# A four-layer graph network on one core: layer 0 issued in single tiles over six block periods, and layers 1 and 3 without split products

## The chip, the cores and the metric

The kernel runs on one core of a Trainium2 chip. The metric is the device time of one execution in microseconds (us), as the median of several runs. The core has five engines that run side by side, each with a queue of its own that it works through in order: TensorE (PE in the profile; its weight loads are PEld), VectorE (DVE), ScalarE (ACT), GpSimd (POOL) and SyncE (SP). DMA transfers are issued from a queue (SP's, or GpSimd's for gathers) and run on 16 DMA engines.

## What is computed

The input is `x`, 2708 nodes of 512 features, and `adj`, a 2708 x 2708 matrix that is nearly empty: a diagonal, and some four other positive entries in a row. Four layers follow one another, each with a residual and a layer normalisation over the 512 features:

```python
x = layernorm(x + (x - (adj @ x) * (diag + 1)) @ W0 + b0)                        # layer 0
x = layernorm(x + sigmoid(gate_a * ((attn @ x) @ W_sa) + gate_b * ((adj @ x) @ W_gc + b)))  # layer 1
x = layernorm(x + ((adj + head) @ x) / rowsum(adj + head))                       # layer 2
x = layernorm(x + tanh((d * (adj + I) * d) @ x @ W3.T + b3))                     # layer 3
```

`attn` is a softmax-like weighting of the same edges (an exponential of leaky scores, divided by its row sum), the gates are sigmoids of sums over the same edges, `head` is a row-normalised mask of them, and `d` is the inverse square root of the column sums. All four layers thus sum neighbours' rows with weights on the same edges. The gates' sums and the scores are linear in `x`, so six extra columns beside each row carry what they need.

## The kernel before

The nodes are cut into 22 blocks of 128 rows (the last has 20). A block of the matrix is loaded transposed, so that a column is a row of `adj`. Layer 0 finds the edges, keeps them for the later layers as a list, and uses them; each block has up to 5 tiles of 128 edges (the last block 1).

**Layer 0**, for a block, in steps (lines 828 to 1052): `load_adj` brings the block's 2708 x 128 matrix into one of two buffers (SP, line 767); `mask` clears the diagonal (GpSimd, 838); `negatives` sums negative entries (ScalarE, 843, two halves); `find` takes the 8 largest values and their places in each of five segments (VectorE, 858 and 859); `number`, `offsets`, `spans`, `places` number the edges; `select` makes a 0/1 matrix on GpSimd (893); `spread_rows` multiplies it on TensorE so that each edge gets its row of candidates (`got`, 904); `keep_rows` copies it out (ScalarE, 917); `pick_edges` picks the edge's value and its neighbour's index (VectorE, 925 to 962); `pick_rows` makes `pick`, a 0/1 matrix in bf16 that says which edge belongs to which row (GpSimd, 971 and 973); `gather_x` fetches the neighbours' rows of `x` by five indirect DMAs (GpSimd, 598) into one of two buffers `xg`; `weigh` multiplies `pick` by the edge values (VectorE 620, its diagonal tile ScalarE 626); `l0_aggregate` sums the rows with these weights on TensorE (995); `add_bias` (GpSimd, 983), `l0_residual` (1002), `l0_u` (VectorE, 1007), a transpose, its copy (680) and `l0_project` (688) give the layer's output; `l0_stats`, `l0_std`, `l0_rstd` and `l0_norm` normalise it (ScalarE's Sqrt at 1026); `x1_transpose`, `x1_copy` and `x1_columns` make the extra columns and store block and columns (SP, 740).

The order is written out by hand. `steps` (1059) gives each step a time within a block, block i is shifted by i times `STEP` = 15, and all steps of all blocks are issued in the order of the sums. These numbers are no waits: they only order each engine's queue, and a semaphore holds an instruction until its data and its buffer are there. A block's steps span 73 units, from the matrix load at -15.5 to the columns at 57.7, all five gathers stand together (26.1), and so do four of the five tile products (35.1).

**Layers 1 to 3** have a common loop (`layer`, 1214): gather the next block, prepare its weights, compute the present block, finish the one before. There a scheduler orders the queues. Layer 1 also gathers one score for each edge (`sl`, line 1121), exponentiates (1142) and makes two weightings of the same rows: `l1a` with the edge values and `l1e` with the attention. Both are transposed and projected with `w_gc` and `w_sa` into one accumulator `l1o` (1199 to 1201).

In layers 1 and 3 most tiles are not multiplied as float32. `split_rows` (634) scales a gathered tile by its edge values into `hi`, rounded to fp32r (ScalarE, 637), and puts the rest into `lo` (VectorE, 639); `picked` (644) makes an fp32r copy of `pick`; `aggregate` (652) then multiplies `pick` by `hi` and by `lo`, two products for a tile:

```python
products = [(s[:, nt, :r], xs[:, i, :D])]
products += [(s[:, t, :r], tiles[:, t, :D]) for t in range(len(parts), nt)]
products += [(pick_s[:, t, :r], x_) for t, pair in enumerate(parts) for x_ in pair]
```

`SPLIT_A, SPLIT_E, SPLIT_3 = 5, 3, 4` are the tiles that are split in `l1a`, `l1e` and `l3a`. The other tiles and the diagonal's are float32 products, as are all of layer 2's. The norms of layers 1 to 3 (`layernorm`, 728) take the inverse root on VectorE by an estimate and two refining steps (`rsqrt`, 710), and layer 1's sigmoids are written with Tanh (1179 and 1207).

## Time and profile before

| What | Value |
|---|---|
| Runs shown | 1240.12, 1244.64, 1236.41 us; median 1240.12 |
| The profiled execution's own time | 1240.12 us |
| Its span, first to last instruction | 1238.4 us, clock 0.918 |
| Busy: TensorE, VectorE, ScalarE, GpSimd | 986.6, 834.2, 524.4, 744.5 us |
| Layer 0's last product (line 1098) starts | 481.4 us |
| Layer 1's projections (`l1o`) | 541.2 to 871.9 us |
| Layer 2's first gathered product, last block's residual (line 1305) | 884.4, 1030.6 us |
| Layer 3's last norm input (line 1346) | 1227 us |

The page lists busy times by engine, then the span in 40 slices, then the chain of work that ended last, then groups of instructions by line. A group gives its count, its busy time, the mean of one, and the idle time of the engine just before it with what ended that. In the order of time of one engine, the bracket behind an instruction is the wait before it and what released it. A float32 matmul stands in the records as two instructions.

### The profile page before, as it was taken

How to read it: one execution, taken by the hardware profiler on the slowest of the kernel's cores; microseconds unless marked ns; L12 is line 12 of the kernel's file. 1: busy time of each engine (PE TensorE's matmuls, PEld its weight loads, DVE VectorE, ACT ScalarE, POOL GpSimd, SP SyncE). 2: the span in 40 equal slices, each digit the busy share in tenths (PEclk: the TensorE clock that was granted, in tenths of full speed). 3: DMA queues.
4: the chain of work that ended last, by engine and by line, in shares of the span. 5: the costliest groups of instructions: out<-in, count | busy, mean ns of one | idle time of the engine just before them, and what ended most of it. 6: DMA issues, size and time to landing. Idle time of an engine off the chain costs nothing.

```text
span 1238.4 us, 12921 instructions
## 1 busy us (share of the span) xinstructions
PE 986.6 (80%) x3074; PEld 502.7 (41%) x3074; DVE 834.2 (67%) x2661; ACT 524.4 (42%) x1033; POOL 744.5 (60%) x787
## 2 busy tenths in 40 slices
PE   0478787777787785379999999999788885799996
PEld 0244344344444442145545555554223332355552
DVE  3677567678566653647767777774487785688885
ACT  1234243343333321446666666664111212666652
POOL 5565565666465642777777777720477775777730
PEclk9989788989788887589999999999899997999998
DMA  8467887787778524222323322310466664566521
GB/s 221 128 119 167 130 168 148 160 138 147 157 146 143 98 51 81 56 78 86 88 80 87 85 83 86 86 54 18 122 185 189 196 197 133 160 198 181 174 90 38
DMA packets 119692, 153.24 MB, mean 124 GB/s; under 512 B 25996, under 2 KB 82864, under 8 KB 119608
## 3 DMA queue, kind: packets, MB, share of 16 engines
q0 software_dynamic: 39024, 95.21, 31.2%
q1 hardware_dynamic: 78472, 57.12, 19.6%
q8 instruction: 26, 0.43, 0.2%
q14 instruction: 58, 0.48, 0.1%
q10 hardware_dynamic: 2112, 0.01, 0.1%
HBM read 152.03 MB, written 22.23 MB: 141 GB/s over the span
## 4 chain that ended last, share of the span: by engine, by line
PE 34%; DMA 15%; issue 7%; DVE 5%; ACT 4%; POOL 3%; POOLq 0%; ACTq 0%; DVEq 0%
PE l1o L688 12%; DMA xg<-x2d,ej 5%; PE l2a L661 5%; PE l1e L661 5%; PE l3o L688 4%; DMA xg<-in_x_dram,ej 3%; DMA xg<-x1d,ej 3%; DMA xg<-x3d,ej 3%; PE l1a L661 2%; POOL xg L598 2%; PE l0a L995 2%; PE l3a L661 2%; ACT hi_s L637 1%; POOL sl L598 1%; DMA x1d<-xs 1%
## 5 line engine op out<-in xcount | busy, mean ns | idle before, releaser
L995 PE MATMUL l0a<-xg,s 128*128 128x512 f32 x212 | 132.4, 749 | 59.8 <-DMA xg<-in_x_dram,ej 59.8
L598 POOL DMA_INDIRECT sl<-sld,er x106 | 127.0, 1199 | 54.0 <-issue 25.6
L598 POOL DMA_INDIRECT xg<-x2d,ej x106 | 114.6, 1081 | 42.5 <-issue 18.0
L598 POOL DMA_INDIRECT xg<-x3d,ej x106 | 114.8, 1083 | 41.5 <-issue 15.8
L598 POOL DMA_INDIRECT xg<-x1d,ej x106 | 110.7, 1044 | 47.2 <-issue 18.9
L598 POOL DMA_INDIRECT xg<-in_x_dram,ej x106 | 111.2, 1049 | 29.1 <-issue 20.8
L661 PE MATMUL l2a<-xg,s2i 128*128 128x512 f32 x212 | 110.3, 638 | 19.2 <-DMA xg<-x2d,ej 18.5
L688 PE MATMUL l1o<-w_gc_sb,uT_l1a 128*128 128x512 f32 (+1 forms) x176 | 88.0, 629 | 15.3 <-ACT uT_l1a L680 15.0
L688 PE MATMUL l3o<-w_sb,uT_l 128*128 128x512 f32 (+1 forms) x176 | 82.6, 613 | 9.4 <-ACT uT_l L680 8.6
L858 DVE MAX8 found<-adj 128x8 f32<-128x512 f32 (+1 forms) x110 | 80.4, 731 | 13.0 <-POOL adj L838 13.0
L995 PEld LDWEIGHTS l0a<-xg,s 128*128 128x128 f32 x212 | 43.8, 234 | 110.1 <-issue 55.5
L639 DVE SCALAR_TENSOR_TENSOR lo_s<-xg,ev,hi_s 128x512 fp32r<-128x512 f32 x85 | 62.9, 743 | 32.6 <-ACT hi_s L637 32.5
L639 DVE SCALAR_TENSOR_TENSOR lo_a<-xg,ev,hi_a 128x512 fp32r<-128x512 f32 x106 | 77.8, 739 | 7.6 <-ACT hi_a L637 5.8
L688 PE MATMUL l0o<-w_sb,uT_l 128*128 128x512 f32 (+1 forms) x176 | 81.3, 604 | 0.7 <-ACT uT_l L680 0.7
L637 ACT ACTIVATE hi_a<-xg,ev 128x512 fp32r<-128x512 f32 x106 | 71.6, 712 | 23.9 <-DMA xg<-x1d,ej 20.8
L859 DVE FIND_INDEX8 index<-found,adj 128x8 uint32<-128x512 f32 (+1 forms) x110 | 81.3, 739 | 0.0
L688 PE MATMUL l1o<-w_sa_sb,uT_l1e 128*128 128x512 f32 (+1 forms) x176 | 79.1, 592 | 0.0
L661 PEld LDWEIGHTS l2a<-xg,s2i 128*128 128x128 f32 x212 | 37.6, 194 | 88.1 <-DMA xg<-x2d,ej 63.7
L904 PE MATMUL got<-found,sel 128*128 128x120 f32 x212 | 41.5, 365 | 36.7 <-POOL sel L893 30.7
L637 ACT ACTIVATE hi_s<-xg,ev 128x512 fp32r<-128x512 f32 x85 | 59.2, 715 | 21.9 <-DMA xg<-x3d,ej 20.4
L893 POOL TENSOR_SCALAR sel<-sel,count 128x640 f32<-128x640 f32 (+1 forms) x22 | 40.8, 1855 | 45.5 <-DVE st_l L698 31.8
L971 POOL CAST ec<-row 128x5 f32<-128x5 uint32 (+1 forms) x22 | 4.1, 189 | 103.2 <-DVE row L954 103.2
(235 smaller groups left out, 2210.9 us busy)
## 6 DMA issues: line engine op xcount, KB each, us to landing
adj<-in_adj_dram SPq DMA_DIRECT2D x21, 1344.0 KB
x1d<-xs SPq DMA_DIRECT2D x21, 257.5 KB
xs<-in_x_dram SPq DMA_DIRECT2D x21, 256.0 KB
x2d<-xs SPq DMA_DIRECT2D x21, 256.0 KB
x3d<-l2y SPq DMA_DIRECT2D x21, 256.0 KB
out_dram<-y SPq DMA_DIRECT2D x21, 256.0 KB
xg<-in_x_dram,ej POOLq DMA_INDIRECT x106, 8.6
xg<-x1d,ej POOLq DMA_INDIRECT x106, 3.6
```

The source lines that it names most:

```text
L598: nc.gpsimd.indirect_dma_start(out=dst, out_offset=None, in_=src[:, :], in_offset=bass.IndirectOffsetOnAxis(ap=index, axis=0), bounds_chec ...
L637: nc.scalar.activation(hi, tiles[:, t, :D], AF.Copy, scale=v)
L639: nc.vector.scalar_tensor_tensor(lo, tiles[:, t, :D], v, hi, op0=ALU.mult, op1=ALU.subtract)
L661: nc.tensor.matmul(agg[:r, :], lhsT=w, rhs=x_, start=k == 0, stop=k == len(products) - 1)
L688: nc.tensor.matmul(o[:r, :], lhsT=uT[:, f, :r], rhs=w[:, f, :], start=start and f == 0, stop=stop and f == DB - 1,)
L858: nc.vector.max(out=best, in_=part)
L859: nc.vector.max_index(index[:, i, 8 * s : 8 * s + 8], best, part)
L893: nc.gpsimd.tensor_scalar(sel[i][:, :m], sel[i][:, :m], count[i][:, SLOTS - 1 : SLOTS], None, op0=ALU.is_lt)
L904: nc.tensor.matmul(got[i][:, t // per_bank, k : k + 3 * SLOTS], lhsT=sel[i][:, t * P : (t + 1) * P], rhs=found[i].rearrange("p a s -> p (a ...
L971: nc.gpsimd.tensor_copy(ec[:, :nt], row[i][:, :nt])
L995: nc.tensor.matmul(agg[i][:r, :], lhsT=weights[i][:, t, :r], rhs=rhs, start=t == 0, stop=t == nt)
```

## The change

Layer 0's table of steps is written anew. `STEP` becomes 15.81 and a block's steps span 105.5 units. Steps are taken apart so that each queue can order them by itself: `gather_x` and `l0_aggregate` are called for one tile at a time, the ScalarE copies of `offsets`, `spans` and `x1_columns` become `keep_offsets`, `keep_values` and `keep_columns`, and the diagonal tile of `weigh` becomes `weigh_diagonal`. Each still does the same. `load_adj` stands at 0 and `mask` directly behind it at 0.1. `select` is issued on VectorE instead of GpSimd. No buffer count of layer 0 changes.

In layers 1 and 3 `split_rows` and `picked` go: every tile is a float32 product with weights from `weighted`. `layernorm` takes ScalarE's Sqrt and VectorE's reciprocal in place of `rsqrt`, and layer 1's two sigmoids are ScalarE's Sigmoid. Left out of the diff below are constants, the names of dictionaries, and the call sites of `l1_compute` and `l3_compute`, which no longer pass the split parts.

```diff
@@ -611,56 +604,40 @@
...
-    def weighted(i, vals, pool, name, diag=None, first=0):
+    def weighted_edges(s, i, vals):
+        r = rows(i)
+        nt = n_tiles(i)
+        nc.vector.tensor_tensor(
+            s[:, :nt, :r],
+            pick[:, i, :nt, :r],
+            vals[:, :nt, None].to_broadcast([P, nt, r]),
+            ALU.mult,
+        )
+    def weighted_diagonal(s, i, vals):
+        r = rows(i)
+        nt = n_tiles(i)
+        nc.scalar.activation(s[:, nt, :r], ident[:, :r], AF.Copy, scale=vals[:, nt : nt + 1])
+    def weighted(i, vals, pool, name, diag=None):
         r = rows(i)
...
         s = pool.tile([P, TILES + 1, P], FP, tag="s", name=name)
-        if first < nt:
-            nc.vector.tensor_tensor(
-                s[:, first:nt, :r],
-                pick[:, i, first:nt, :r],
-                vals[:, first:nt, None].to_broadcast([P, nt - first, r]),
-                ALU.mult,
-            )
-        nc.scalar.activation(
-            s[:, nt, :r],
-            ident[:, :r],
-            AF.Copy,
-            scale=vals[:, nt : nt + 1] if diag is None else diag,
-        )
+        weighted_edges(s, i, vals)
+        if diag is None:
+            weighted_diagonal(s, i, vals)
+        else:
+            nc.scalar.activation(s[:, nt, :r], ident[:, :r], AF.Copy, scale=diag)
         return s
-    def split_rows(pool, tiles, t, v, name):
-        hi = pool.tile([P, D], FR, tag="hi", name=f"hi_{name}_{t}", bufs=n_parts)
-        nc.scalar.activation(hi, tiles[:, t, :D], AF.Copy, scale=v)
-        lo = pool.tile([P, D], FR, tag="lo", name=f"lo_{name}_{t}", bufs=n_parts)
-        nc.vector.scalar_tensor_tensor(
-            lo, tiles[:, t, :D], v, hi, op0=ALU.mult, op1=ALU.subtract
-        )
-        return hi, lo
-    def picked(pool, i):
-        r = rows(i)
-        nt = n_tiles(i)
-        s = pool.tile([P, TILES, P], FR, tag="pick", name=f"pick{i}")
-        nc.vector.tensor_copy(s[:, :nt, :r], pick[:, i, :nt, :r])
-        return s
-    def aggregate(pool, i, s, tiles, tag, name, pick_s=None, parts=()):
+    def aggregate(pool, i, s, tiles, tag, name):
         r = rows(i)
...
         agg = pool.tile([P, D], FP, tag=tag, name=name)
-        products = [(s[:, nt, :r], xs[:, i, :D])]
-        products += [(s[:, t, :r], tiles[:, t, :D]) for t in range(len(parts), nt)]
-        products += [(pick_s[:, t, :r], x_) for t, pair in enumerate(parts) for x_ in pair]
-        for k, (w, x_) in enumerate(products):
-            nc.tensor.matmul(
-                agg[:r, :], lhsT=w, rhs=x_, start=k == 0, stop=k == len(products) - 1
-            )
+        for t in range(nt + 1):
+            rhs = tiles[:, t, :D] if t < nt else xs[:, i, :D]
+            nc.tensor.matmul(agg[:r, :], lhsT=s[:, t, :r], rhs=rhs, start=(t == 0), stop=(t == nt))
         return agg
@@ -707,32 +684,11 @@
...
-    def rsqrt(y, a, r, name):
-        k = small.tile([P, 4], FP, tag="newton", name=f"nw_{name}")
-        bits = small.tile([P, 1], U32, tag="bits", name=f"bits_{name}")
-        nc.vector.tensor_scalar(
-            bits[:r, :], a.bitcast(U32), 1, None, op0=ALU.logical_shift_right
-        )
-        y0, t, y1, q = (k[:r, j : j + 1] for j in range(4))
-        nc.vector.tensor_scalar(
-            y0.bitcast(U32), bits[:r, :], -1.0, float(GUESS), op0=ALU.mult, op1=ALU.add
-        )
-        nc.vector.scalar_tensor_tensor(t, y0, a, y0, op0=ALU.mult, op1=ALU.mult)
-        nc.vector.scalar_tensor_tensor(t, t, -10.0 / 3.0, t, op0=ALU.add, op1=ALU.mult)
-        nc.vector.scalar_tensor_tensor(y1, t, 5.0, y0, op0=ALU.add, op1=ALU.mult)
-        nc.vector.scalar_tensor_tensor(q, y1, a, y1, op0=ALU.mult, op1=ALU.mult)
-        nc.vector.scalar_tensor_tensor(q, q, -64.0 / 3.0, y1, op0=ALU.add, op1=ALU.mult)
-        nc.vector.tensor_scalar(y, q, -27.0 / 1024.0, None, op0=ALU.mult)
...
         mv = norm_stats(v, r, name)
-        nc.vector.tensor_scalar(mv[:r, 1:2], mv[:r, 1:2], 1e-5, None, op0=ALU.add)
         rstd = small.tile([P, 2], FP, tag="rstd", name=f"rs_{name}")
-        rsqrt(rstd[:r, 0:1], mv[:r, 1:2], r, name)
-        nc.vector.scalar_tensor_tensor(
-            rstd[:r, 1:2], mv[:r, 0:1], -1.0, rstd[:r, 0:1], op0=ALU.mult, op1=ALU.mult
-        )
+        nc.scalar.activation(rstd[:r, 0:1], mv[:r, 1:2], AF.Sqrt, bias=eps_ln[:r, :])
+        norm_scale(rstd, mv, r)
         nc.scalar.activation(dst, v, AF.Identity, bias=rstd[:r, 1:2], scale=rstd[:r, 0:1])
...
@@ -875,12 +831,17 @@
...
         nc.tensor.matmul(ps[:, 1:2], lhsT=before2, rhs=n, start=True, stop=True)
-        nc.scalar.copy(offs[:, i, :], ps[:, 0:2])
+        offs_ps[i] = ps
+    def keep_offsets(i):
+        nc.scalar.copy(offs[:, i, :], offs_ps[i][:, 0:2])
...
+    def keep_values(i):
         nc.scalar.copy(value[:, i, :], found[i][:, 1, :])
@@ -890,7 +851,7 @@
...
         m = n_tiles(i) * P
-        nc.gpsimd.tensor_scalar(
+        nc.vector.tensor_scalar(
             sel[i][:, :m], sel[i][:, :m], count[i][:, SLOTS - 1 : SLOTS], None, op0=ALU.is_lt
...
@@ -974,27 +933,33 @@
...
-    def gather_x(i):
-        gather(i, x, D)
+    def gather_x(i, t):
+        if t < n_tiles(i):
+            gather_rows(xg_buf[i % 2][:, t, :D], x, ej[:, i, t : t + 1])
...
+    def weigh_diagonal(i):
+        weights[i] = spool.tile([P, TILES + 1, P], FP, tag="s", name=f"s0_{i}")
+        weighted_diagonal(weights[i], i, ev[:, i])
     def weigh(i):
-        weights[i] = weighted(i, ev[:, i], spool, f"s0_{i}")
-    def l0_aggregate(i, first, last):
+        weighted_edges(weights[i], i, ev[:, i])
+    def l0_aggregate(i, t):
         r = rows(i)
         nt = n_tiles(i)
-        if first == 0:
+        if t == 0:
             agg[i] = psg.tile([P, D], FP, tag="agg", name=f"l0a{i}")
-        for t in range(first, min(last, nt + 1)):
-            rhs = xg_buf[i % 2][:, t, :D] if t < nt else xs[:, i, :D]
-            nc.tensor.matmul(
-                agg[i][:r, :], lhsT=weights[i][:, t, :r], rhs=rhs, start=t == 0, stop=t == nt
-            )
+        if t > nt:
+            return
+        rhs = xg_buf[i % 2][:, t, :D] if t < nt else xs[:, i, :D]
+        nc.tensor.matmul(
+            agg[i][:r, :], lhsT=weights[i][:, t, :r], rhs=rhs, start=t == 0, stop=t == nt
+        )
@@ -1042,12 +1007,15 @@
...
         r = rows(i)
-        cols = psg.tile([P, 6], FP, tag="off", name=f"cols{i}")
+        cols[i] = psg.tile([P, 6], FP, tag="off", name=f"cols{i}")
         for f in range(DB):
             nc.tensor.matmul(
-                cols[:r, :], lhsT=xT[i][:, f, :r], rhs=w6[:, f, :], start=f == 0, stop=f == DB - 1
+                cols[i][:r, :], lhsT=xT[i][:, f, :r], rhs=w6[:, f, :], start=f == 0, stop=f == DB - 1
             )
-        nc.scalar.copy(xs[:r, i, D:], cols[:r, :])
+    def keep_columns(i):
+        r = rows(i)
+        nc.scalar.copy(xs[:r, i, D:], cols[i][:r, :])
         store(x1d, i, xs[:r, i, :XG])
@@ -1055,20 +1023,23 @@
-    STEP = 15
+    STEP = 15.81
     steps = (
-        (-15.5, load_adj), (-2, load_x), (2.7, mask),
-        (3.6, find, 0), (5.5, find, 1), (11, find, 2), (12.6, find, 3), (14.2, find, 4),
-        (6.2, negatives, 0), (7.6, negatives, 1),
-        (15.8, number), (16.5, offsets), (16.8, spans), (16.9, places), (17.6, select),
-        (18.7, spread_rows), (20.2, keep_rows), (21.9, pick_edges), (24.2, pick_rows),
-        (26.1, gather_x), (31.9, weigh), (32.8, l0_aggregate, 0, 1), (34, add_bias),
-        (35.1, l0_aggregate, 1, TILES + 1), (39.5, l0_residual), (39.6, l0_u),
-        (41, l0_transpose), (41.7, l0_copy), (42.7, l0_project), (47.7, l0_stats), (48.6, l0_std),
-        (50.2, l0_rstd), (50.4, l0_norm), (55.4, x1_transpose), (55.8, x1_copy), (57.7, x1_columns),
+        (0, load_adj), (0.1, mask), (11.4, negatives, 0), (13.9, find, 0), (14.9, negatives, 1),
+        (15.8, find, 1), (18.8, find, 2), (20, load_x), (20.5, find, 3), (26.7, find, 4),
+        (27.5, keep_values), (30, number), (32.8, offsets), (33.6, keep_offsets), (33.9, spans),
+        (34.3, places), (36.3, select), (36.4, spread_rows), (37.6, keep_rows),
+        (42.5, pick_edges), (43.1, gather_x, 0), (45.7, pick_rows), (47.6, gather_x, 1),
+        (52.3, add_bias), (53.5, weigh_diagonal), (56.9, gather_x, 2), (63.1, gather_x, 3),
+        (65.8, weigh), (68.7, l0_residual), (71.2, gather_x, 4), (72.6, l0_aggregate, 0),
+        (74.2, l0_aggregate, 1), (78.7, l0_aggregate, 2), (81.1, l0_aggregate, 3),
+        (82.2, l0_aggregate, 4), (83.1, l0_aggregate, 5), (84.5, l0_u), (88.8, l0_transpose),
+        (89.7, l0_copy), (91, l0_project), (95.2, l0_stats), (96.1, l0_std), (97.4, l0_rstd),
+        (98.3, l0_norm), (99.7, x1_transpose), (103.4, x1_copy), (104.6, x1_columns),
+        (105.5, keep_columns),
     )
     plan = [(i * STEP + s[0], i, s[1], s[2:]) for i in range(NB) for s in steps]
-    plan.append((16.2, 0, lambda i: score_weights(), ()))
+    plan.append((40, 0, lambda i: score_weights(), ()))
     with tc.manual_schedule():
...
@@ -1175,18 +1144,13 @@
...
-        nc.scalar.activation(g[:r, 0:2], g[:r, 0:2], AF.Tanh, scale=0.5)
-        nc.vector.tensor_scalar(g[:r, 0:2], g[:r, 0:2], 0.5, 0.5, op0=ALU.mult, op1=ALU.add)
+        nc.scalar.activation(g[:r, 0:2], g[:r, 0:2], AF.Sigmoid)
         nc.vector.tensor_scalar(g[:r, 2:3], sums[:r, 2:3], 1e-5, None, op0=ALU.add)
...
         nc.vector.tensor_mul(g[:r, 2:3], g[:r, 2:3], g[:r, 0:1])
-        na, ne = min(nt, SPLIT_A), min(nt, SPLIT_E)
-        parts_a = [split_rows(w1p, tiles, t, ev[:, i, t : t + 1], f"a{i}") for t in range(na)]
-        parts_e = [split_rows(w1p, tiles, t, e[:, 2, t : t + 1], f"e{i}") for t in range(ne)]
-        sv = weighted(i, ev[:, i], spool, f"s1v{i}", first=na)
-        se = weighted(i, e[:, 2], w1p, f"s1e{i}", first=ne)
-        return sv, se, g, picked(w1p, i), parts_a, parts_e
+        sv = weighted(i, ev[:, i], spool, f"s1v{i}")
+        se = weighted(i, e[:, 2], w1p, f"s1e{i}")
+        return sv, se, g
@@ -1203,11 +1167,8 @@
...
-        nc.scalar.activation(v[:r, :], v[:r, :], AF.Tanh, scale=0.5)
-        nc.vector.scalar_tensor_tensor(
-            v[:r, :], v[:r, :], 0.5, xs[:r, i, :D], op0=ALU.mult, op1=ALU.add
-        )
+        nc.scalar.activation(v[:r, :], v[:r, :], AF.Sigmoid)
+        nc.vector.tensor_add(v[:r, :], v[:r, :], xs[:r, i, :D])
         layernorm(xs[:r, i, :D], v[:r, :], r, f"l1_{i}")
...
@@ -1329,11 +1290,7 @@
...
     def l3_prepare(i, tiles):
-        nt = n_tiles(i)
-        n3 = min(nt, SPLIT_3)
-        parts = [split_rows(w3p, tiles, t, ev[:, i, t : t + 1], f"s{i}") for t in range(n3)]
-        s = weighted(i, ev[:, i], spool, f"s3_{i}", diag=dd3[:, i : i + 1], first=n3)
-        return s, picked(w3p, i), parts
+        return weighted(i, ev[:, i], spool, f"s3_{i}", diag=dd3[:, i : i + 1])
```

More of the change, by code (lines that the diff above doesn't have):

```diff
@@ L436 @@
 FAR = 1 << 22
-GUESS = 0x5F3759DF
-SPLIT_A, SPLIT_E, SPLIT_3 = 5, 3, 4
 @with_exitstack
@@ L494, in sparse_path @@
     BF = mybir.dt.bfloat16
-    FR = mybir.dt.float32r
     N, D = x.shape
@@ L833, in sparse_path @@
     found, valid, count, sel, rowsets, xb, weights = {}, {}, {}, {}, {}, {}, {}
-    agg, u, uT, o, xT, mv, rstd, got = {}, {}, {}, {}, {}, {}, {}, {}
+    agg, u, uT, o, xT, mv, rstd, got, offs_ps, row, cols = ({} for _ in range(11))
     def mask(i):
@@ L964, in pick_edges @@
         )
-    row = {}
     def pick_rows(i):
@@ L1114, in sparse_path @@
     bg_bc = load_row(c1, b_gc, "bg_bc")
-    n_parts = 10
     def l1_gather(i):
@@ L1227, in l1_compute @@
     def l1_compute(i, tiles, ready, finish_before):
-        sv, se, g, pick_s, parts_a, parts_e = ready
-        agg_a = aggregate(psl, i, sv, tiles, "agg", f"l1a{i}", pick_s, parts_a)
+        sv, se, g = ready
+        agg_a = aggregate(psl, i, sv, tiles, "agg", f"l1a{i}")
         if finish_before is not None:
             finish_before()
-        agg_e = aggregate(psl, i, se, tiles, "agg", f"l1e{i}", pick_s, parts_e)
+        agg_e = aggregate(psl, i, se, tiles, "agg", f"l1e{i}")
         return lambda: l1_finish(i, g, agg_a, agg_e)
@@ L1353, in l3_compute @@
     def l3_compute(i, tiles, s, finish_before):
-        s, pick_s, parts = s
-        agg = aggregate(ps3, i, s, tiles, "agg", f"l3a{i}", pick_s, parts)
+        agg = aggregate(ps3, i, s, tiles, "agg", f"l3a{i}")
         if finish_before is not None:
```

## The prediction

> **What bounds the kernel now.** I read the page's head and slices first, then busy time by stretch, then the order of time of single engines inside a stretch, and the waits last. The slices show four layers with different limits (each digit is tenths of a slice of 31 us).
>
> ```profile
> span 1238.4 us, 12921 instructions
> ...
> PE   0478787777787785379999999999788885799996
> ...
> DVE  3677567678566653647767777774487785688885
> ...
> POOL 5565565666465642777777777720477775777730
> PEclk9989788989788887589999999999899997999998
> ```
>
> Layer 0 fills slices 0 to 15, layer 1 16 to 27, layer 2 28 to 32, layer 3 the rest. In layer 0 no engine is full. In layer 1 and most of layer 3 TensorE is.
>
> ```profile
> 100.00:440.00 340.00, 261.30 (x883) 142.54 (x882) 232.48 (x595) 120.34 (x254) 201.63 (x234) 0.87 0.75 141
> 565.00:845.00 280.00, 273.27 (x945) 150.23 (x944) 200.47 (x824) 176.53 (x357) 181.13 (x159) 1.00 0.28 80
> 890.00:1020.00 130.00, 112.42 (x239) 41.32 (x237) 100.23 (x310) 25.22 (x53) 101.61 (x94) 0.96 0.65 188
> 1095.00:1200.00 105.00, 104.08 (x331) 56.25 (x330) 89.89 (x267) 70.83 (x125) 70.66 (x65) 1.00 0.56 164
> ```
>
> The columns are TensorE, weight load, VectorE, ScalarE, GpSimd, clock, DMA share, GB/s; the rows are the steady parts of layers 0 to 3. TensorE is busy 98% in layer 1 and 99% in layer 3, at full clock. In layer 2 five gathers of 1.08 us plus 0.30 us of issue each, 6.9 us, equal the block period of 7 us: GpSimd's issue sets it. Layer 0 has 77, 68 and 59% on TensorE, VectorE, GpSimd: a loop of waits sets it, seen on TensorE and GpSimd in order of time.
>
> ```profile
> 414.76 2.05 PE L995 MATMUL l0a<-xg,s 128*128 128x512 f32 x2 [6.53 <-DMA xg<-in_x_dram,ej]
> ...
> 434.23 2.49 PE L904 MATMUL got<-found,sel 128*128 128x120 f32 x10 [2.04 <-POOL sel L893]
> ```
>
> ```profile
> 250.44 1.89 POOL L893 TENSOR_SCALAR sel<-sel,count 128x640 f32<-128x640 f32 x1 [5.12 <-DVE st_l L698]
> ...
> 257.34 0.19 POOL L971 CAST ec<-row 128x5 f32<-128x5 uint32 x1 [3.37 <-DVE row L954]
> ...
> 260.71 1.43 POOL L598 DMA_INDIRECT xg<-in_x_dram,ej  x1 [0.16 <-PE l0o L1002]
> ```
>
> The loop: got on TensorE (252.4), row copies, edge picking, five gathers (260.7 to 267.4), their landing (8.6 us median in this layer), the aggregate (271.6 to about 279), projection, then the next-but-one block's offsets, selection and got: some 39 us for two blocks. The starts of the bias addition (line 983) run from 53.59 to 450.94 over 20 blocks: 19.87 us a block. Layer 0 ends at 481.8.
>
> Layer 1's matmuls in order of time give the prices:
>
> ```profile
> 696.96 0.40 PE L661 MATMUL l1a<-lo_a,pick 128*128 128x512 f32 x1
> 697.19 0.39 PE L661 MATMUL l1a<-hi_a,pick 128*128 128x512 f32 x1
> ...
> 705.54 3.60 PE L688 MATMUL l1o<-w_sa_sb,uT_l1e 128*128 128x512 f32 x8
> 708.97 1.88 PE L661 MATMUL l1e<-xg,s1e 128*128 128x512 f32 x4
> ...
> 718.15 2.84 PE L688 MATMUL l1o<-w_gc_sb,uT_l1a 128*128 128x512 f32 x6 [1.02 <-ACT uT_l1a L680]
> ```
>
> Start to start, an fp32r product takes 0.23 us; a float32 product is two records, eight records take 3.43 us, so 0.86 us. The last line is the one wait that layer 1 leaves TensorE.
>
> **What the Trainium skill says.** *FP8 and Floating Point Precision*, TensorE Precision Notes: true FP32 takes four passes of the array. The trace agrees: 0.86 over 0.23 is 3.7. *ScalarE: Activation LUTs*, Table sets: exp and tanh share a set, sigmoid and sqrt head others. The trace agrees: layer 1 with Exp and Tanh alone shows no table load between 518 and 840 us. The same page, What ACT_TABLE_LOAD costs: 1283 ns and a drain of 1380 ns a switch. The trace has the first and not the second, and I use its 1.28:
>
> ```profile
> 511.31 1.28 ACT L1256 ACT_TABLE_LOAD   x1
> 512.61 0.22 ACT L1256 ACTIVATE d_inv<-d_inv 128x22 f32<-128x22 f32 x1
> ```
>
> *DMA: Bandwidth & Descriptors*, Issuing engines are not separate DMA queues: transfers of all queues interleave on the same 16 engines. The trace agrees: gathers land in 8.6 us beside the adjacency loads of layer 0, and in 3.7 us in layer 2; a load's 2708 packets of 512 B lie within 5.5 us alone (29.25 to 34.70) and within 9 to 13 us beside gathers.
>
> **Layer 1: the split is undone.** Five tiles of the one aggregate and three of the other go from two fp32r products (0.46) to one float32 product (0.86): 8 x 0.40 = 3.2 us a block on TensorE, which is the bound, x 21 = +67 us. What leaves, eight scaled copies on ScalarE (0.715) and eight subtractions (0.74) and a cast (0.49) on VectorE, lay beside it and gives little: those engines had 63 and 72%. One place does wait for it, the start: TensorE stood 8.45 us until 541.2 for a transposed copy queued on ScalarE behind a scaled copy that waited for a gather. I take -5 there; nothing to the whole wait is possible. Tanh becomes Sigmoid and the square root returns to ScalarE, so each block switches tables up to three times (exp, sigmoid, sqrt): 3.85 us on an engine that falls to some 5 of 19 us. It costs if a load stands ahead of the transposed copies that end TensorE's wait; bounds 0 and 1.28 x 21 = 27 us for one such load a block, and I take half, +13. Layer 1: +75.
>
> **Layer 3.** Four tiles x 0.40 x 21 = +34. At the start TensorE waited 2.93, 2.84 and 2.01 us for transposed copies behind scaled ones; I take -4. Tanh and Sqrt alternate, two loads a block, 2.6 us on ScalarE whose other work is then about 3.3 of 9.4 us; TensorE has 1.7 us of other products between transposes and projection, which covers one, so I take 0 (27 without this cover). Layer 3: +30.
>
> **Layer 2.** Nine VectorE instructions of 0.147 to 0.216 us, 1.49 us a block, become a 0.28 us ScalarE root and a 0.145 us reciprocal. VectorE isn't the bound; gathers stretch from 1.00 to 1.08 us beside it, so at most 5 x 0.08 x 21 = 8. I take -4.
>
> **Layer 0.** Selection moves: 1.9 us leave GpSimd, and 640 elements on VectorE by the 0.511 us row of 512 (line 1310) cost 0.64. Summed start to start for one block, VectorE then has 14.8 us, TensorE 14.0, GpSimd about 11.7. So no engine forbids 15 us; the question is the loop that the new order leaves. The plan's times only sort each queue. In its order GpSimd's mask of block p stands directly before gather 1 of p-3, the bias of p-3 and gather 4 of p-4, and waits for p's adjacency load. Then: load issue to landing 10.5, mask 0.45, gather 1.3, bias 1.2, gather 1.1, its landing about 8, two products 1.9, the two operations of l0_u 1.4, pick_edges 2.6, the last find 1.4, and some 3 of hops (semaphores and descriptor start) until the load of block p+2 goes out. That is 33 us for two blocks, 16.5 each; with 5 us less of DMA 14, with the 3 us later landings seen 18. I take 16.8. Behind the blocked mask stand all five gathers and the row picks of a period (11.2 us), which fit in the rest of it. On ScalarE the two negatives (1.6 us each) wait for the same landing; ahead of them stand the copies of blocks p-5 and p-6, behind them block p-1's values and p-6's root (0.28 us), which VectorE needs 3 us later. On SP a block's x load (256 KB) now goes out 4 us after the next block's adjacency load and is read 32 us later; the stores of p-6, which stood directly ahead of a load, stand mid-period and hold the next load up only if the columns are 4 us late.
>
> The end: VectorE's queue up to block 0's statistics holds 65 us of work from 20.5, so about 88 with waits; from there to the last find are 16.67 periods; after that TensorE has some 50 us left (19 of aggregates, 20 of transposes and projections, 7 of columns, small waits), 53. 88 + 16.67 x 16.8 + 53 = 421 against 481.8: -61 us.
>
> **Sum.** -61 + 75 - 4 + 30 = +40 on a span of 1238.4; the profiled execution's own 1240.12 has 1.7 us around it and equals the median of the runs. **1280 us.**
>
> **Rivals.** (a) *The blocked mask sets a slow loop.* With the longest load (13.3) and gather landing (13.9) of this trace the loop is 41 us and the period 20: layer 0 gains nothing, 1341 us. For it: GpSimd, idle for 40% of layer 0, gets a new wait at the head of each period. Against: such landings are the worst ones. (b) *Table loads stand on TensorE's path*, one whole load a block in layers 1 and 3: +14 and +27, 1320 us. For it: the 1.02 us wait on the transposed copy is there already. Against: ScalarE loses half its work. (c) *VectorE alone sets layer 0*, never waiting: 88 + 16.67 x 14.84 + 53 = 388, a gain of 94, 1247 us, not slower. It decides from a period of about 15.1 us on. For it: the order spreads each latency over several periods. Against: it leaves no room for a late landing in a 33 us loop. That float32 products hide in layers 1 and 3 has at most their 2% of idle TensorE time.
>
> **How the numbers follow.** Forecast 0.60 with its own range 1262 to 1302; (a) 0.12, (b) 0.10, (c) 0.13; 0.05 lies outside all. One per cent, 12.4 us, is about what can be told from no change. (c) reaches below 1252 in most of its cases and below 1228 in few: faster 0.04, same 0.09, slower 0.87. The range 1250 to 1320 leaves out (a) and the lower part of (c).
>
> **What would show it.** Right: layer 0 ends near 421 with 16 to 17.5 us between bias additions; in layer 1 about 19 to 19.6 us between projections (15.7 now), TensorE at 97% or more, and no fp32r line; in layer 3 9.4 us a block (7.8 now); some five table loads a block over layers 1 and 3. Wrong: TensorE waits over 1.5 us a block for transposed copies (b), GpSimd's mask waiting while TensorE waits for gathers (a), or layer 0 below 395 us (c).

## The result and the profile after

The changed kernel took 1312.28 us (median of four runs, 1307.56 to 1313.96), beside 1240.81 us for the kernel before on the same chip: a ratio of 1.057, with an interval of 1.053 to 1.062. The profiled execution took 1307.56 us with a span of 1305.8 us, 67.4 us longer than before's span. First the head and the slices (each now 33 us).

```profile
span 1305.8 us, 11459 instructions
...
PE   0277876767878836999998999999688886999996
...
DVE  4989777779777343333333333332366662333333
...
POOL 5465456545467057555455455410477775755540
PEclk9999988889889967999999999999799998999998
```

Layer 0 fills slices 0 to 14, and TensorE is at 6 to 8 tenths there, as before. Then the busy time of the four steady parts, in the columns of the prediction's table (TensorE, weight load, VectorE, ScalarE, GpSimd, clock, DMA share, GB/s):

```profile
100.00:440.00 340.00, 262.39 (x952) 140.77 (x950) 258.91 (x629) 121.12 (x262) 183.77 (x228) 0.89 0.74 140
565.00:845.00 280.00, 264.61 (x759) 121.22 (x758) 95.15 (x412) 132.07 (x230) 147.58 (x144) 1.00 0.25 71
945.00:1075.00 130.00, 108.09 (x233) 36.96 (x231) 83.29 (x163) 30.31 (x71) 102.14 (x92) 1.00 0.66 186
1120.00:1280.00 160.00, 160.00 (x427) 73.93 (x427) 56.21 (x124) 101.18 (x141) 85.45 (x84) 1.00 0.49 142
```

In layers 1 and 3 VectorE has lost half its work, but TensorE is still the full engine: it has more to do for each block. In layer 1 it fell from 98 to 94.5% busy, so there is a wait that was not there. The 67.4 us come together so (starts of the same instruction in both traces):

| Stretch | Before | After | Difference |
|---|---|---|---|
| Start to layer 0's last product | 481.4 | 464.8 | -16.6 |
| From there to layer 1's first residual input | 69.9 | 60.6 | -9.3 |
| Layer 1, first to last residual input | 320.6 | 394.2 | +73.6 |
| To layer 3's first | 195.7 | 194.0 | -1.7 |
| Layer 3, first to last | 159.7 | 182.1 | +22.4 |
| To the end | 11.1 | 10.1 | -1.0 |

So layer 0 gave much less than the 61 us forecast, and layers 1 and 3 cost less than forecast. The bias additions of layer 0 show how: for the first four blocks they are 14.2 to 15.3 us apart, and then mostly alternate between about 15 and 24 us (starts 198.75, 214.50, 238.25). The chain of waits in order of time, cut to one such pair of blocks, names the pieces (start, length, what):

```profile
196.88 0.06 POOL adj L794
...
198.75 1.27 POOL xb L943
200.02 0.16 issue
200.18 10.29 DMA xg<-in_x_dram,ej
210.46 0.04 issue
210.51 3.52 PE l0a L960 x4
...
220.27 15.97 DMA adj<-in_adj_dram
...
236.39 0.06 POOL adj L794
```

GpSimd's mask (L794) ends its wait at 196.88 and again at 236.39: 39.5 us for two blocks. Between them lie the bias addition, one gather with its landing, the products, and the next-but-one matrix load. Between 214 and 220 the chain that the profile prints goes through TensorE and another gather, which the load does not need. What the load does wait for is VectorE's last search of the buffer that it overwrites: here and two blocks later it goes out 0.06 to 0.07 us after that search's end. In VectorE's order of time:

```profile
214.06 0.69 DVE L972 TENSOR_TENSOR l0u<-l0a,ndiag 128x512 f32<-128x512 f32 x1 [6.25 <-PE l0a L960]
214.79 1.37 DVE L973 TENSOR_TENSOR l0u<-l0u,xs 128x512 f32<-128x512 f32 x1
216.09 0.35 DVE L886 TENSOR_TENSOR hit<-rowsets,edge_no 128x200 f32<-128x200 f32 x1
...
219.52 0.69 DVE L815 FIND_INDEX8 index<-found,adj 128x8 uint32<-128x512 f32 x1
220.12 0.81 DVE L814 MAX8 found<-adj 128x8 f32<-128x640 f32 x1
```

VectorE stands 6.25 us for the late aggregate; `pick_edges` and the block's last search queue behind it, and the search ends at 220.2, when the load may overwrite its buffer. The waits between 100 and 380 us (engine, line, what released it: total, times, longest) hold the same four places:

```profile
POOL adj L794 <- DMA adj<-in_adj_dram: 102.2, 13, 16.7
...
PE l0a L960 <- DMA xg<-in_x_dram,ej: 46.8, 7, 8.5
...
DVE l0u L972 <- PE l0a L960: 34.9, 7, 6.3
...
DVE found L814 <- DMA adj<-in_adj_dram: 12.0, 6, 6.5
```

### The profile page after: what moved, and what is told of

Read it like the earlier page. It is cut to its first block, busy times and chain, and to the rows that moved or that the text cites. A ratio compares the mean times of both kernels' runs of the same rounds, so it can differ in the third digit from the quotient of the medians.

```text
span 1305.8 us, 11459 instructions
## 1 busy us (share of the span) xinstructions
PE 1051.3 (81%) x3074; PEld 487.2 (37%) x3074; DVE 667.9 (51%) x1858; ACT 525.0 (40%) x953; POOL 688.0 (53%) x765
## 4 chain that ended last, share of the span: by engine, by line
PE 31%; DMA 26%; issue 17%; POOL 12%; DVE 11%; ACT 2%; POOLq 1%; DVEq 0%; SPq 0%; ACTq 0%
PE l3a L640 8%; DMA adj<-in_adj_dram 7%; DMA xg<-x2d,ej 6%; POOL xg L591 6%; PE l3o L665 6%; DMA xg<-x1d,ej 5%; DMA xg<-in_x_dram,ej 5%; POOL sl L591 4%; PE l0a L960 4%; PE l1o L665 3%; DVE index L815 2%; PE l2a L640 2%; DVE found L814 2%; PE l0o L665 2%; PE got L865 1%
## 5 line engine op out<-in xcount | busy, mean ns | idle before, releaser
L960 PE MATMUL l0a<-xg,s 128*128 128x512 f32 x212 | 117.8, 652 | 49.5 <-DMA xg<-in_x_dram,ej 48.8
L591 POOL DMA_INDIRECT sl<-sld,er x106 | 110.6, 1043 | 83.5 <-DVE e L1109 53.1
L591 POOL DMA_INDIRECT xg<-x3d,ej x106 | 108.0, 1019 | 67.4 <-PE l3a L640 47.6
L591 POOL DMA_INDIRECT xg<-in_x_dram,ej x106 | 112.4, 1060 | 46.2 <-issue 19.3
L640 PE MATMUL l1e<-xg,s1e 128*128 128x512 f32 x212 | 100.0, 602 | 12.4 <-DVE s1e L611 12.4
L640 PE MATMUL l3a<-xg,s 128*128 128x512 f32 x212 | 100.3, 603 | 11.2 <-DMA xg<-x3d,ej 11.2
L640 PE MATMUL l1a<-xg,s1v 128*128 128x512 f32 x212 | 96.9, 602 | 8.6 <-DMA xg<-x1d,ej 8.3
L794 POOL TENSOR_TENSOR adj<-adj,not_ident 128x128 f32<-128x128 f32 x22 | 10.0, 457 | 135.4 <-DMA adj<-in_adj_dram 127.3
L799 ACT ACTIVATE minus<-adj 128x1408 bf16<-128x1408 f32 x44 | 60.6, 1377 | 35.0 <-POOL adj L794 19.2
L1167 DVE SCALAR_TENSOR_TENSOR l1v<-bg_bc,g,l1o 128x512 f32<-128x512 f32 (+1 forms) x22 | 16.4, 746 | 102.8 <-PE l1o L665 102.8
L932 POOL TENSOR_SCALAR pick<-iota_c,ec 128x128 bf16<-128x128 f32 x106 | 64.2, 620 | 2.2
```

The lines of the kernel that those rows point to most:

```text
L591: nc.gpsimd.indirect_dma_start(out=dst, out_offset=None, in_=src[:, :], in_offset=bass.IndirectOffsetOnAxis(ap=index, axis=0), bounds_chec ...
L640: nc.tensor.matmul(agg[:r, :], lhsT=s[:, t, :r], rhs=rhs, start=(t == 0), stop=(t == nt))
L794: nc.gpsimd.tensor_tensor(a[:, i, :], a[:, i, :], not_ident, ALU.mult)
L799: nc.scalar.activation(minus, abuf[i % 2][:, k * half : (k + 1) * half, :], AF.Relu, scale=-1.0, accum_out=neg[:, i, k : k + 1],)
L932: nc.gpsimd.tensor_scalar(pick[:, i, t, :], iota_c, ec[:, t : t + 1], None, op0=ALU.is_equal)
L960: nc.tensor.matmul(agg[i][:r, :], lhsT=weights[i][:, t, :r], rhs=rhs, start=t == 0, stop=t == nt)
```

## The experiments

**Theory 1**, for layer 0: the mask on GpSimd, blocked until its matrix is there, holds the older blocks' gathers; these make the aggregate late, that makes VectorE's last search late, and that the load of two blocks on. **Rival:** gathers and matrix loads simply share the DMA engines, and where the mask stands does not matter. Ratios are to the kernel before, run beside each kernel on its chip, with 95% intervals; the kernel before took 1231.2 us beside the first four, 1231.56 beside the next four and 1257.45 beside the last three. None of the kernels leaves out a part of the computation.

**The new layer 0 alone** (`l0_alone`): the changed kernel with `split_rows`, `rsqrt` and Tanh of before put back.

```diff
-        sv, se, g = ready
-        agg_a = aggregate(psl, i, sv, tiles, "agg", f"l1a{i}")
+        sv, se, g, pick_s, parts_a, parts_e = ready
+        agg_a = aggregate(psl, i, sv, tiles, "agg", f"l1a{i}", pick_s, parts_a)
...
```

> The kernel before with the new layer 0 only; layers 1 to 3 keep the split products, the Newton root and Tanh. If the parts add up as the two traces read (layer 0's end 16.6 us earlier, some of it a shorter start of layer 1): 1240 - 17 = about 1224 us, layer 0's last product at 465 as in the changed kernel, two-block loop of 39 us again. If the new layer 0 helped or hurt layer 1 (its start fell by 9.3 us), the time is 1215 (the start's gain belongs to layer 0) or 1224 to 1233 (it belongs to the removal of the split).

Measured: 1215.2 us, 0.989 (0.982 to 0.996). Layer 0's last product starts at 457.9 us, the alternation is there (14.2, 25.1, 14.0, 23.2), and the first residual input of layer 1 follows 67.8 us later, as before: the shorter start belongs to the removal of the split (`rest_alone`, which lacks the split, has 60.6).

**The rest alone** (`rest_alone`): the changed kernel with the old table of steps and the selection on GpSimd.

```diff
-    STEP = 15.81
+    STEP = 15
...
-        nc.vector.tensor_scalar(
+        nc.gpsimd.tensor_scalar(
             sel[i][:, :m], sel[i][:, :m], count[i][:, SLOTS - 1 : SLOTS], None, op0=ALU.is_lt
```

> The changed kernel with the old layer 0; layers 1 to 3 have float32 products, Sqrt and Sigmoid. Parts that add up: 1312 + 17 = about 1329 us (1240 + 74 of layer 1's blocks - 9 of its start - 2 of layer 2 + 22 of layer 3 is 1325 to 1334). If layers 1 to 3 owe part of their +88 to what layer 0 leaves behind (queues not yet drained), less: 1315 to 1322.

Measured: 1305.71 us, 1.063 (1.056 to 1.070), under what was expected for parts that add up and within what was expected otherwise. But the two ratios multiply to 1.051, which the intervals do not separate from the 1.057 of the whole, so neither is shown. Here the old layer 0 ended at 465.1 us, 16 us earlier than in the trace of before, and the new one, unchanged, at 457.8 to 464.8 us in four traces: one trace of layer 0 varies by as much as the change gained in it.

**The mask issued later** (`mask_later`).

```diff
-        (0, load_adj), (0.1, mask), (11.4, negatives, 0), (13.9, find, 0), (14.9, negatives, 1),
+        (0, load_adj), (11.3, mask), (11.4, negatives, 0), (13.9, find, 0), (14.9, negatives, 1),
```

> The changed kernel with one number other: GpSimd's mask of a block is issued at 11.3 instead of 0.1, directly ahead of gather 0 of block p-2 and behind gather 1, the bias, gather 4 and gather 2 of the older blocks. Theory 1, the blocked mask holds the gathers of older blocks until the matrix is there, and they then collide with nothing but each other while TensorE waits: the two-block alternation of 15 and 24 us goes, 15 to 16.5 us a block, layer 0's last product at 400 to 425, time 1250 to 1272 us. Rival, gathers and matrix loads share the DMA engines and the mask's place does not matter: layer 0's end within 8 us of 465 and the time within 1304 to 1320 us.

Measured: 1272.46 us, 1.033 (1.026 to 1.040). Layer 0 ends at 437.2; blocks are 17.0 us apart on average, still uneven (12 to 23), and GpSimd still waits for matrices, less. The rival's 465 is out; theory 1's direction holds and its size does not quite.

**The mask on VectorE** (`mask_vector`), ahead of the search that waits for the same load.

```diff
-        nc.gpsimd.tensor_tensor(a[:, i, :], a[:, i, :], not_ident, ALU.mult)
+        nc.vector.tensor_tensor(a[:, i, :], a[:, i, :], not_ident, ALU.mult)
...
-        (0, load_adj), (0.1, mask), (11.4, negatives, 0), (13.9, find, 0), (14.9, negatives, 1),
+        (0, load_adj), (11.3, mask), (11.4, negatives, 0), (13.9, find, 0), (14.9, negatives, 1),
```

> The changed kernel with the mask on VectorE directly ahead of the block's first search, which waits for the same load anyway; GpSimd then waits for no matrix. It costs VectorE about 0.2 us a block. Theory 1, the blocked mask on GpSimd sets the loop: 15 to 16 us a block, layer 0's last product at 400 to 420, time 1248 to 1268 us. Rival, contention on the DMA engines alone: layer 0's end at 465 to 475 and 1310 to 1322 us.

Measured: 1270.71 us, 1.032 (1.025 to 1.038). Layer 0 ends at 435.1, 29.7 us before the changed kernel's. The alternation is all but gone: from the fifth block to the 17th, 16.4 to 17.7 us from one to the next. Period and time are a little above the ranges expected, and far from the rival's. Busy time in its layer 0:

```profile
100.00:380.00 280.00, 238.46 (x866) 137.18 (x867) 250.65 (x616) 116.19 (x247) 162.38 (x197) 0.90 0.81 163
```

VectorE has 90%, more than any other engine. The DMA engines are busier (0.81 against 0.79 in the same stretch of the changed kernel), and a load still takes as long (its last packet ends 15.7 us after its issue, 15.3 in the changed kernel). So the loads did not become faster; they left the loop that set the pace.

**A third matrix buffer** (`third_buffer`), the mask left where it was.

```diff
-    abuf = [c0.tile([P, NB, P], FP, name=f"adj{k}") for k in range(2)]
+    abuf = [c0.tile([P, NB, P], FP, name=f"adj{k}") for k in range(3)]
...
-        (0, load_adj), (0.1, mask), (11.4, negatives, 0), (13.9, find, 0), (14.9, negatives, 1),
+        (-15.81, load_adj), (0.1, mask), (11.4, negatives, 0), (13.9, find, 0), (14.9, negatives, 1),
```

> The changed kernel with three matrix buffers instead of two and load_adj one block period earlier in the order (at -15.81); the mask stays on GpSimd at 0.1. Theory 1 (the loop last find, load, blocked mask, gathers, aggregate, last find): the load no longer waits for the last find but one, the mask finds its matrix landed, the alternation of 15 and 24 us goes without any new work on VectorE, 15 to 16.5 us a block, layer 0's last product at 405 to 432, ratio to the kernel before 1.01 to 1.03 (1243 to 1268 us where before is 1231). Rival, contention of gathers with matrix loads on the DMA engines sets the landings: the loads only start earlier beside other gathers, alternation stays, ratio 1.05 to 1.065.

Measured: 1276.54 us, 1.037 (1.031 to 1.043). Layer 0 ends at 434.1, its blocks are 16.8 to 17.4 us apart from the fifth to the 17th, and between 100 and 380 us GpSimd has no wait for a matrix among its largest. The loop is cut at another place and gives the same gain: theory 1 stands. The total is a little above the range expected, since the period is 16.7 us and not 15 to 16.5.

**The selection behind the blocked mask** (`select_gpsimd`).

```diff
-        nc.vector.tensor_scalar(
+        nc.gpsimd.tensor_scalar(
             sel[i][:, :m], sel[i][:, :m], count[i][:, SLOTS - 1 : SLOTS], None, op0=ALU.is_lt
```

> The changed kernel with the selection on GpSimd, at the place in the order that it has. VectorE loses 0.53 us a block, GpSimd gains 1.9 us between its mask and its gathers. If the loop over the blocked mask sets layer 0, the 1.9 us come on top of the loop's gathers once in two blocks: layer 0's end 15 to 25 us later, ratio 1.07 to 1.08. If GpSimd's time doesn't matter (contention or VectorE sets it): layer 0's end within 8 us of 465 or earlier, ratio 1.045 to 1.062.

Measured: 1429.16 us, 1.161 (1.154 to 1.167): far more than either side expected. GpSimd and TensorE in order of time:

```profile
271.72 0.45 POOL L794 TENSOR_TENSOR adj<-adj,not_ident 128x128 f32<-128x128 f32 x1 [10.97 <-DMA adj<-in_adj_dram]
272.49 1.05 POOL L591 DMA_INDIRECT xg<-in_x_dram,ej  x1 [0.32 <-issue]
273.59 1.90 POOL L854 TENSOR_SCALAR sel<-sel,count 128x640 f32<-128x640 f32 x1
...
275.55 0.78 PE L865 MATMUL got<-found,sel 128*128 128x120 f32 x2 [11.04 <-POOL sel L854]
```

The mask waits 10.97 us for a matrix, the selection of an older block stands behind it, and TensorE waits 11.04 us for that. `pick_edges` and the searches on VectorE wait in turn, for every block: the bias additions are 23.6 us apart on average (58.3 to 554.3 us). So in this order the selection's move to VectorE is no side matter: it takes the most urgent step out from behind the wait.

**No table loads in layers 1 to 3** (`no_switch`): the changed kernel with `rsqrt` and Tanh of before.

```diff
-        nc.scalar.activation(g[:r, 0:2], g[:r, 0:2], AF.Sigmoid)
+        nc.scalar.activation(g[:r, 0:2], g[:r, 0:2], AF.Tanh, scale=0.5)
+        nc.vector.tensor_scalar(g[:r, 0:2], g[:r, 0:2], 0.5, 0.5, op0=ALU.mult, op1=ALU.add)
...
-        nc.scalar.activation(rstd[:r, 0:1], mv[:r, 1:2], AF.Sqrt, bias=eps_ln[:r, :])
-        norm_scale(rstd, mv, r)
+        rsqrt(rstd[:r, 0:1], mv[:r, 1:2], r, name)
...
```

> The changed kernel with the Newton root on VectorE and Tanh for the sigmoids, so that ScalarE loads hardly a table in layers 1 to 3; float32 products stay. If table loads cost what the prediction gave them (13 us of layer 1, 0 in layer 3), layer 1 falls from 19.5 to about 18.9 us a block, layer 2 is 4 us longer: ratio to the kernel before about 1.05. If they stand wholly beside TensorE's work: 19.5 and 9.0 us a block as before, ratio 1.055 to 1.062. If one whole load a block stands on the path in both layers: ratio 1.02 to 1.035.

Measured: 1324.72 us, 1.076 (1.070 to 1.082), slower than with them. Table loads fall from 116 to 7, layer 1 goes from 19.2 to 20.2 us a block (blocks 2 to 20), layer 3 stays at 9.0. None of the expectations had this sign. The run exchanges two things at once, so it does not price the loads alone: whatever they cost in layer 1 is about 1 us a block less than what the small VectorE operations cost that stand in for Sqrt and Sigmoid. In the waits of layer 1 (600 to 880 us) of this kernel, the edge sums' wait for VectorE is

```profile
PE sums L1152 <- DVE e L1148: 25.8, 14, 3.0
```

and was 15.5 us in 14 times in the changed one: 0.7 us more a block, most of the difference.

**A third buffer for gathered rows** (`xg_third`). That wait led to a second theory. In the changed kernel's order of time (all engines):

```profile
700.86 1.01 POOL L591 DMA_INDIRECT xg<-x1d,ej  x1 [3.44 <-PE l1e L640]
...
710.23 0.17 DVE L1099 COPY q<-xg 128x15 f32<-128x15 f32 x1 [6.67 <-DMA xg<-x1d,ej]
...
713.65 0.29 PE L1129 MATMUL sums<-e,pick 128*128 128x15 bf16 x5 [2.75 <-DVE e L1125]
```

A gather waits until the float32 products have read the buffer, the scores wait for its landing, TensorE for the sums.

```diff
-    xg_buf = [const.tile([P, TILES, XG], FP, name=f"xg{k}") for k in range(2)]
+    xg_buf = [const.tile([P, TILES, XG], FP, name=f"xg{k}") for k in range(3)]
...
-        g = xg_buf[i % 2]
+        g = xg_buf[i % 3]
```

> The changed kernel with three buffers instead of two for the gathered rows in layers 1 to 3 (layer 0 keeps using two). New theory for layer 1's 0.6 us a block beyond the products: a float32 product reads the gathered rows themselves, so a buffer is held until the last product of a block, where the split had copied most tiles out; the next gathers, and the score gathers queued behind them, go out late, and TensorE waits 1.1 us a block ahead of the edge sums. Then the wait goes with the third buffer: 19.5 us a block becomes 18.4 to 18.9, layer 1 shorter by 12 to 23 us, ratio to the kernel before 1.037 to 1.047. Rival, the order of GpSimd's queue or VectorE's own row of small operations makes the sums late: 19.4 to 19.6 us a block, ratio 1.052 to 1.062.

Measured: 1336.13 us, 1.060 (1.053 to 1.068): a ratio in the rival's range, and not told apart from the changed kernel's 1.057. Between 620 and 880 us TensorE's busy time is

```profile
620.00:880.00 260.00, 252.77 (x725) 114.73 (x724) 90.62 (x401) 140.81 (x236) 123.75 (x121) 1.00 0.23 68
```

against 245.53 us in the changed kernel, and its wait for the sums is gone, as the theory said. But it is partly replaced by waits for copies behind the exponential on ScalarE (11.3 us of weight load in nine times), and a block takes 18.9 us, where the other kernels with float32 products and Sqrt had 18.9 to 19.3. That is some 6 us of layer 1 at most, and in this run layer 3 lost more at its start (21.4 us for one block). Layers 2 and 3 are also longer than elsewhere in `best_third` and `best_third_sel`, which ran beside the same slower kernel before, so not all of that need be the buffer's doing. The wait's cause is shown; that its removal is worth anything is not.

**Towards a better kernel.** Layers 1 to 3 of before with the new layer 0 and each cure: `best_vector` (mask on VectorE), `best_third` (third matrix buffer, earlier load) and `best_third_sel` (the latter, with the selection on GpSimd). The edits are those above, put together.

> The kernel before (split products, Newton root, Tanh) with the new layer 0 and its mask on VectorE. If the parts add up: the new layer 0 alone was 0.989 of before and the mask's move took some 30 us: about 0.965 of before, 1188 us where before is 1231; layer 0's last product at 435. If layer 1's gathers or its start take it back: 0.975 to 0.99.

> The kernel before with the new layer 0 and its third matrix buffer (loads one period earlier, mask on GpSimd). If the third buffer does for this kernel what it did for the changed one: layer 0's last product at 434, ratio 0.965 to 0.975 (1188 to 1201 us where before is 1231), as with the mask on VectorE. If the longer DMA use takes it back: 0.98 to 0.99.

> As best_third, with the selection on GpSimd as in the kernel before. With the changed kernel's order this cost 128 us; theory: because the selection stood behind a mask that waited for its matrix. With the matrix there in time the selection costs nothing on the path and takes 0.53 us a block off VectorE, which then sets layer 0: 16.2 to 16.7 us a block, layer 0's end 424 to 436, ratio 0.955 to 0.975. If GpSimd's own 1.9 us a block (and VectorE waiting for its port) were what made it slow: 18 us a block or more, ratio 0.99 or above.

Measured: 1197.07 us, 0.971 (0.964 to 0.979); 1216.29 us beside a before of 1257.45, 0.969 (0.962 to 0.976); and 1186.07 us on that same chip, 0.942 (0.937 to 0.948). The first two are close to what was expected of parts that add up; the third is below every range expected. In it layer 0 ends at 404.0 us and its blocks are 15.3 us apart. Its busy time there:

```profile
100.00:380.00 280.00, 254.45 (x952) 143.15 (x950) 239.93 (x612) 120.53 (x261) 211.81 (x244) 0.96 0.84 165
```

The move of the selection to GpSimd, which cost a tenth with the mask blocked (1.161 against 1.057), takes 2.7% off once the matrix is there in time (0.942 against 0.969). The period falls by 1.5 us, though the selection takes VectorE only 0.59 us. A second saving can be seen: one small VectorE operation of every block (that of 128 x 1 numbers in the last section) takes 0.86 us on average in `best_third` between 110 and 350 us, and 0.16 us in all its 15 instances here. The two together make 1.3 of the 1.5 us, as they would if VectorE's row of work set the period of `best_third`. TensorE, VectorE and GpSimd now have 91, 86 and 76%, at a DMA share of 0.84, as high as in any of these kernels. This kernel is faster than both the kernel before and the changed one.

## Why the prediction was right, and where it failed

The direction was right: the float32 products of layers 1 and 3 cost more than the new layer 0 gives. Point by point:

- **Layer 0, -61: measured -16.6. The term that failed is the load in the loop**, "load issue to landing 10.5". It was 15.97 us (220.27 to 236.25). The rest of the loop measured 23.5 against 22.5 in the sum, with errors that cancel: the gather's landing, the two products and `l0_u` took some 3.5 us more, and of the 3 us allowed for hops hardly any was needed. So two blocks took 39.5 us, not 33. In the forecast's own sum for the end, 88 was 92.9, 53 was 55.4, and the period of 16.8 was 19.0 on average over 16.67 blocks; the period alone is 36.7 of the 44 us missed. The change did not make the load that long: 10.5 was too short for the kernel before as well. In its trace, from 84 us on, the last packet of a load ends 12.7 to 16.3 us after the issue, 14.6 on average. What does last some 10.5 us there is the issuing instruction on SP's queue (last section); whether the forecast took its figure from that is not on record. With 14.6 in place of 10.5 its sum gives 18.5 us a block. It also put the length of these loads down to the gathers beside them, which the traces contradict (last section again). What the forecast called rival (a), a loop of 41 us, is what the steady part of layer 0 did; its sign, the mask waiting while TensorE waits for gathers, is in the waits. The three cures confirm the mechanism.
- **Rival (c), VectorE alone at 14.84.** Its row of work was too short as well. With the mask out of the way the period is 16.7 to 16.8 us, and by `best_third_sel` it is VectorE that sets it: some of its short operations wait for GpSimd (last section).
- **Layer 1, +75: measured +73.6 and -9.3.** The products' +67 is right: a block took 3.63 us more (15.58 to 19.21, blocks 2 to 20) against 3.2 for the products. The +13 for table loads found no support: the kernel without them is slower, by what replaces them, and their own price stays open. The remainder of 7 us goes with a new wait for the edge sums, which the prediction did not have: "what leaves ... gives little" missed that the split's copies also let go of the gathered rows early. At the start, -5 was -9.3; TensorE's wait of 8.45 us there became 6.96, so the rest of the gain lies elsewhere in the start and was not traced.
- **Layer 2, -4: measured +5.3.** The table's -1.7 joins two parts. From layer 1's last residual input to layer 2's, 158.8 us became 164.1; from there to layer 3's first, 36.9 became 29.9. No trace has the gain that was forecast. Leaving out the three runs beside the slower kernel before, layer 2 takes 158.8 to 160.5 us in the kernels with the old layers 1 to 3 and 161.6 to 164.5 in those with the new. `no_switch` has 164.5 with the old root, so the root is not the cause; what is stays open.
- **Layer 3, +30: measured +22.4, and -7.1 at its start, where -4 was forecast.** The period went from 7.7 to 9.0 us, 1.3 where four tiles at 0.40 make 1.6. The kernel before had a small wait of TensorE for a transposed copy ahead of its projections there (0.28 us before the one at 1129.40; 10.7 us in 13 times on the weight load between 1100 and 1200 us), which went with the scaled copies. The forecast had credited such waits to the start alone. Table loads at 0 were right: TensorE is busy for 160.00 of 160 us.
- **The sum.** +40 forecast, +67 measured: 44 us missed in layer 0, some 17 us too much in the others. The two errors partly cancel, so that it is luck that the time fell inside the range of 1250 to 1320; it is above the 1262 to 1302 of the likeliest case.

## What to carry to other kernels

An instruction that waits for a load blocks everything behind it in its queue, whatever the table of times says: put it on an engine whose next work needs the same load, or load one buffer further ahead. When a loop of waits contains a transfer, cost it from issue to landing and in the steady part of the trace: the issuing instruction and the first transfers of the kernel can both be shorter. And when a copy goes away, ask which buffer it used to free early.

## What the runs showed of the hardware

**Matrix loads that double once stores go out.** In the changed kernel's order of time on SP's queue (L723 loads a block's matrix, L786 its rows of `x`; L696 stores a finished block and its scores):

```profile
89.04 2.71 SPq L723 DMA_DIRECT2D adj<-in_adj_dram  x1
91.79 0.35 SPq L786 DMA_DIRECT2D xs<-in_x_dram  x1
103.10 0.34 SPq L696 DMA_DIRECT2D x1d<-xs  x1
103.49 0.44 SPq L696 DMA_DIRECT2D sld<-xs  x1
104.04 0.38 SPq L720 DMA_DIRECT2D adj<-in_adj_dram  x1
104.47 9.10 SPq L723 DMA_DIRECT2D adj<-in_adj_dram  x1
```

The load issued at 88.56 us has its last packet 6.7 us later, the one at 104.04, the first behind a store of a finished block, 14.2 us later. It is so in all 13 traces: from the third matrix load on, those issued before the first store take 6.1 to 8.2 us to the last packet, and all behind it 11.7 to 18.1. Gathers do not explain it: up to five go out beside the short loads too. The issuing instruction grows too: 2.71 us became 9.10 here, and in the kernel before, between 100 and 380 us, it is as long (shortest, median and longest in ns):

```profile
L767 SPq DMA_DIRECT2D adj<-in_adj_dram x14: 9051/10684/12234, 107.7 to 369.5; - x14
```

In the changed kernel the blocks begin to alternate just when the loads become long. No run moved the stores, so whether the stores themselves or something that begins with them lengthens the loads is not shown.

**Short VectorE operations that wait inside themselves.** In the kernel with the mask on VectorE an operation on 128 x 1 numbers, 0.16 us elsewhere, takes 1.90 us; all engines in order of time:

```profile
248.48 1.90 DVE L683 SCALAR_TENSOR_TENSOR rs_l<-mv_l,rs_l 128x1 f32<-128x1 f32 x1
...
249.08 1.27 POOL L943 TENSOR_TENSOR xb<-xs,b_bc 128x512 f32<-128x512 f32 x1
```

It ends at 250.38, GpSimd's addition at 250.35. Of its instances between 110 and 370 us, all 14 that meet that addition end within 0.03 us of its end, and the two that don't meet it take 0.16 us. The Trainium skill, *SBUF — State Buffer*, SBUF: two separate sides, says that VectorE and GpSimd share a port pair under an exclusive lock, also for a VectorE operation with two SBUF inputs against a GpSimd one that reads SBUF. The trace agrees. It adds a case: the operation begins up to 0.6 us ahead of the addition and still ends with it. But a meeting does not always cost so much: in the kernel before, nine of 13 such operations (110 to 370 us) begin 0.38 us ahead of the addition, take 0.43 to 0.44 us and end just after its start. What decides is not shown. No wait stands in the profile for it; it is to be found by an instruction longer than its like. With the third matrix buffer two such operations took 0.71 and 0.77 us a block, start to start, where they take 0.08 and 0.17 undisturbed: 1.2 us of a period of 16.7, which is most of what the forecast's 14.84 for VectorE's row lacked.

**Table loads without a visible price.** The changed kernel has 116 of them, 1.28 us each, and in layer 3 TensorE is busy for 160.00 of 160 us beside them. The Trainium skill, *ScalarE: Activation LUTs*, What ACT_TABLE_LOAD costs, adds a longer drain to each. It is not seen here: at 714.70 us a load begins and the next operation starts at 715.99.
